# A graph network's lone column group as a 2x2 block product of seven half-width products

## The chip, the cores and the metric

The kernel runs on one core of one Trainium2 chip. The metric is device time of one execution in microseconds (us). The kernel before takes 461.95 us, the median of 3 runs (461.89 to 461.96).

## The reference

2500 nodes with 256 features, 80000 edges sorted by their end node, three layers. Each layer takes, for every node, the mean over its incoming edges of a linear map of (own features, neighbour minus own), and a relu; a last linear map joins the input and the three layers' outputs.

```
h = relu(layernorm(x));  xs = [h]
for W, b in three layers:
    m = concat([h[dst], h[src] - h[dst]]) @ W + b       # 80000 x 512 by 512 x 256
    s = segment_sum(m, dst);  cnt = segment_sum(1, dst)
    h = relu(s / max(cnt, 1));  xs.append(h)
out = x + concat(xs) @ Wf + bf
```

Since m is linear, the kernel never forms it by edge. With A the matrix of counts (how many edges go from node i to node j), s is A-transposed times z, with z = (h W_b) scaled by node, plus h times (W_t - W_b) for nodes that have edges. So a layer is a small product per node (z, and the layer's share of the last map), and a large one with A, 2560 by 2500.

## The kernel before

**Tiles.** Nodes lie in 20 tiles of 128, two of which make one of Q = 10 steps (q). The columns of A (end nodes) are in 5 groups: four of 504 columns, and group 4, `alone`, of 486. Features stand on the partitions in `hT` (256 = 2 x 128 rows, by node). z is held in two parts, `zh` and `zl`, whose sum has the precision of F32; each product with A is done with both, in TensorE's fast F32 form. `sh` and `sl` hold sums of the four 128 x 128 blocks of z, made by `combine` (three DVE operations `tmp<-tmp`) and `Nodes.sums` (ACT's `sh`, DVE's `sl`).

**Layer 0** builds A while it multiplies: the units of group g (`layer`, one per tile of 128, plus four `own` units in between with the product of hT and its own weight) run on TensorE, while group g+1 is compared and counted (`compare`, `counts`, `take_counts`; loop of lines 1120 to 1160). When a group's A is complete, `finish` (lines 903 to 913) adds one row from `cnt` and POOL stores A as bf16 to `a_dram[g]`. `by_count` (915 to 920) scales hT by the counts and, for groups 2 to 4, lets `split_own` (1082 to 1088) split the group's first own factor in three parts: ACT the high one, DVE the low and the cross one. Group 4 builds nothing; in its units `shares` (717 to 737) counts all edges found, by DVE's `fewer` and `found` and one tiny matmul `bank<-ones,found`, and `first_forms` (1094 to 1106) prepares layer 1.

**Layers 1 and 2** (lines 1423 to 1488) have two stages. The *lone stage* goes through the ten q: `Nodes` (1207 to 1239) makes z for two tiles by 12 matmuls of 512 columns from three parts of hT made two steps ahead (`Split`: ACT's `staged<-hT`, then two DVE `staged`); `parts` scales (ACT `tmp` twice), takes the high part (ACT `zh`), the low one (DVE `zl`) and adds the share of the last map to `acc` (DVE, twice). Two steps behind, `Alone.multiply` (1333 to 1371) multiplies z of that step with group 4's columns: 8 matmuls of 486 columns, of a block loaded as bf16 from `a_dram[4]` and cast by ACT (`block<-staged`). Four plain F32 matmuls bring group 4's own part, two of them at the end. The *stream* (`Stream.run`, 1405 to 1413) then multiplies groups 0 to 3, as two pairs (`Pair`, 1246 to 1331). A pair is a 2x2 block product by seven products in place of eight (`SEVEN`): b11, b21, b22 are blocks of A, r1 to r4 sums of blocks that DVE makes (r1 to r2 are cast by ACT after that). Each of 5 chunks gives seven steps of four matmuls of 504 columns, with blocks made LEAD = 5 steps ahead. `take` brings the seven results together.

**What sets the order.** Each engine does its instructions in the order in which the code issues them, and each waits by semaphore for the operands of others, and for those who still read what it overwrites. SP issues the loads, in order too. Nothing is reordered later, so the order of the calls in the loops is the schedule.

## Time and profile before

| | |
|---|---|
| median of 3 runs | 461.95 us (461.89 to 461.96) |
| profiled execution | 461.73 us, of which the span of its instructions is 459.8 |
| group 4 of layer 0, first product | 169.0 us |
| nodes of layer 1, first product | 190.41 us |
| first product of the stream, layer 1 | 238.76 us |
| nodes of layer 2, first product | 315.2 us |
| first product of the stream, layer 2 | 363.57 us |
| last map alone, first product | 439.91 us |
| busy: TensorE / VectorE / ScalarE | 452.0 / 373.7 / 313.0 us |

PE is TensorE's matmul, PEld its weight load, DVE VectorE, ACT ScalarE, POOL GpSimd, SP the engine that issues most transfers. A row of the timeline gives start, duration, engine, line, operation, the names out<-in, the shape and how many, and in brackets how long the engine was idle before it and whom it waited for. The recorded duration of a matmul holds its tail, so the price of one is taken from start to start. A row of stretches gives the busy us of PE, PEld, DVE, ACT and POOL with the number of instructions, then the granted clock of TensorE, the share of the DMA engines and GB/s. Most rows bear line 282, a helper's that records every operation, so places are told by names.

### The profile page before, as it was taken

The numbers are of one execution on the slowest core, as the hardware profiler recorded it, in microseconds if no ns is written. First come the engines' busy times: TensorE is split into PE (matmuls) and PEld (weight loads), VectorE is DVE, ScalarE is ACT, GpSimd is POOL, SyncE is SP. The second block draws the span as 40 slices with busy tenths as digits, with TensorE's granted clock in tenths as the row PEclk, the third lists the DMA queues.
The fourth block names the chain that finished last, engine by engine and source line by source line (L and its number), as shares of the span: only waits on it lengthen the run. The fifth ranks groups of instructions, "written<-read, shape, count | busy, mean of one in ns | idle before, by whom it ended". The sixth has DMA issues, their size and how long they took to land.

```text
span 459.8 us, 7427 instructions
## 1 busy us (share of the span) xinstructions
PE 452.0 (98%) x2729; PEld 356.6 (78%) x2729; DVE 373.7 (81%) x720; ACT 313.0 (68%) x575; POOL 41.6 (9%) x75
## 2 busy tenths in 40 slices
PE   8999999999999999999999999999999999999995
PEld 4888877677778778878878868877788787688685
DVE  7999979899888946199979859886999687569795
ACT  4879878694945434387779839756877897497540
POOL 4770006101001010000000000000000000000000
PEclk9999999999999999999999999999999999999999
DMA  8320088982908249211396522011114855220014
GB/s 273 103 59 13 1 171 133 204 172 42 185 1 168 60 95 189 92 45 45 95 362 235 188 92 91 0 45 46 45 50 138 332 181 180 90 91 0 1 63 165
DMA packets 21784, 52.20 MB, mean 114 GB/s; under 512 B 1915, under 2 KB 12110, under 8 KB 21742
## 3 DMA queue, kind: packets, MB, share of 16 engines
q1 hardware_dynamic: 14110, 33.31, 21.9%
q0 software_dynamic: 5856, 16.48, 18.6%
q10 hardware_dynamic: 1776, 1.89, 1.2%
q8 instruction: 22, 0.36, 0.3%
q14 instruction: 20, 0.16, 0.1%
HBM read 36.21 MB, written 15.62 MB: 113 GB/s over the span
## 4 chain that ended last, share of the span: by engine, by line
PE 96%; DVE 3%; issue 0%; DVEq 0%
PE bank L282 87%; PE pz L282 8%; PE turned L282 1%; DVE one_n L282 1%; DVE one_m L282 1%; DVE own_h L282 0%; DVE hT L282 0%; DVE pick L282 0%; DVE behind L282 0%; DVE deg L282 0%; DVE acc L282 0%; DVE idle L516 0%; DVE acc L431 0%; DVE away L282 0%; DVE deg_b L282 0%
## 5 line engine op out<-in xcount | busy, mean ns | idle before, releaser
L282 ACT CAST block<-staged 128x1008 fp32r<-128x1008 bf16 x120 | 118.0, 1032 | 16.5 <-DVE staged L282 6.5
L282 PE MATMUL bank<-block,zh 128*128 128x504 f32 (+1 forms) x200 | 83.8, 419 | 0.0
L282 PE MATMUL bank<-a,zh 128*128 128x504 f32 (+1 forms) x200 | 82.0, 410 | 0.0
L282 PE MATMUL bank<-a,zl 128*128 128x504 f32 (+1 forms) x200 | 77.8, 389 | 0.0
L282 PE MATMUL bank<-block,zl 128*128 128x504 f32 (+1 forms) x200 | 77.3, 387 | 0.0
L282 ACT CAST a<-bank 128x480 fp32r<-128x480 f32 (+1 forms) x105 | 54.3, 561 | 31.3 <-PE bank L282 31.1
L282 DVE TENSOR_TENSOR one_m<-iota_m,key_m 128x2048 bf16<-128x2048 bf16 (+2 forms) x55 | 64.0, 1164 | 9.4 <-PE bank L282 9.1
L282 PE MATMUL bank<-block,sh 128*128 128x504 f32 x160 | 68.9, 430 | 0.0
L282 PE MATMUL bank<-block,staged 128*128 128x512 f32 (+1 forms) x288 | 62.8, 369 | 0.0
L282 PE MATMUL bank<-block,sl 128*128 128x504 f32 x160 | 62.6, 391 | 0.0
L282 PEld LDWEIGHTS bank<-block,staged 128*128 128x128 f32 x288 | 49.4, 188 | 10.2 <-issue 0.7
L282 DVE TENSOR_TENSOR block<-staged 128x1008 fp32r<-128x1008 bf16 x40 | 46.9, 1204 | 5.2 <-PE bank L282 3.9
L282 PEld LDWEIGHTS bank<-block,zh 128*128 128x128 f32 x200 | 37.6, 188 | 10.9 <-issue 2.5
L282 PEld LDWEIGHTS bank<-block,zl 128*128 128x128 f32 x200 | 37.6, 188 | 10.7 <-issue 3.2
L282 PEld LDWEIGHTS bank<-a,zh 128*128 128x128 f32 x200 | 37.7, 188 | 6.6 <-ACT a L282 0.3
L282 PEld LDWEIGHTS bank<-a,zl 128*128 128x128 f32 x200 | 37.8, 189 | 6.2 <-issue 0.2
L282 DVE TENSOR_TENSOR one_n<-iota_n,key_n 128x640 bf16<-128x640 bf16 (+2 forms) x110 | 42.4, 427 | 0.0
L282 PEld LDWEIGHTS <-one_m 128*128 128x128 bf16 x834 | 30.3, 98 | 13.8 <-issue 7.3
L282 PE MATMUL pz<-wbf,hT 128*128 128x256 f32 x160 | 38.3, 385 | 0.0
L282 PEld LDWEIGHTS bank<-block,sh 128*128 128x128 f32 x160 | 30.1, 188 | 10.3 <-issue 3.5
L282 PEld LDWEIGHTS bank<-block,sl 128*128 128x128 f32 x160 | 30.1, 188 | 9.4 <-issue 3.7
L282 DVE TENSOR_TENSOR staged<-staged 128x1008 bf16<-128x1008 bf16 x40 | 27.1, 678 | 12.0 <-ACT block L282 11.6
(190 smaller groups left out, 633.6 us busy)
## 6 DMA issues: line engine op xcount, KB each, us to landing
staged<-a_dram SPq DMA_DIRECT2D x52, 504.0 KB, 4.4
a_dram<-a POOLq DMA_DIRECT2D x20, 630.0 KB, 9.9
acc<-in_x_dram POOLq DMA_DIRECT2D x3, 640.0 KB, 12.0
out_dram<-acc SPq DMA_DIRECT2D x5, 256.0 KB, 2.2
acc<-in_x_dram SPq DMA_DIRECT2D x2, 512.0 KB
wbf<-in_L_gnn_Wf_dram SPq DMA_DIRECT2D x3, 256.0 KB
acc<-in_x_dram ACTq DMA_DIRECT2D x1, 768.0 KB
wt<-in_L_gnn_W_dram SPq DMA_DIRECT2D x3, 256.0 KB
```

Of the source, the lines that this page charges most:

```text
L282: return self.tc.keep_in_program_order(call(*args, **kwargs))
```

## The change

Group 4's product in layers 1 and 2 becomes a 2x2 block product too, by the same seven products. Its 486 columns are cut into halves of H = 244 (they overlap by two columns), so that a step q has 14 matmuls of 244 columns in place of 8 of 486.

The seven blocks of each q are made once, in layer 0, and kept in DRAM as F32 (`lone_dram`, 976 bytes a row and block): b11, b21, b22 by three transfers that ACT issues in `finish(4)`, the four sums by DVE (`sums_of_alone`), each q's stored by SP. Four of the ten q are done before group 4's products, three of them ahead of `split_own(4, 0)`, the others at odd units of group 4. The sums lie in the buffers of `one_m` and `one_n` in turn, later also in two of their own; each of these must be stored before it is used again. The bf16 copy of group 4, the clearing of its last columns and the ACT casts of its blocks go.

In the lone stage each q's seven blocks (854 KB) are loaded straight to where the matmuls read them. `combine` of the weights and the four sums of hT are made ahead of the stage; the seven own products come at steps 0 and 1. `sums` of a step is issued at the start of the next step, ahead of its `parts`; before, it was behind them. The last of the ten products with group 4 and `end` (the seven `take`) move into the stream, at its step HOLD = 3. `Nodes` uses four banks in turn in place of six. The bodies of `own_sum` and `take` move unchanged from `Pair` to a class `Sevens` that both share.

```diff
-    a_dram = [dram.tile([P, NT, GS], BF16, name=f"a_dram{g}") for g in range(NG)]
+    a_dram = [dram.tile([P, NT, GS], BF16, name=f"a_dram{g}") for g in range(alone)]
+    H = (GWS[alone] * W + 3) // 4 * 2
+    SECOND = slice(GWS[alone] * W - H, GWS[alone] * W)
+    lone_dram = dram.tile([P, Q, 7, H], F32, name="lone_dram")
...
     def finish(g, a):
         c0, n = group_of(g)
-        if n < GS:
-            DVEo.memset(a[:, :, n:].bitcast(F32), 0.0)
         ACTo.copy(a[PAD:PAD + 1, NT - 1, :n], cnt[PAD:PAD + 1, c0:c0 + n])
-        for t in range(0, NT, 5):
-            POOLo.dma_start(a_dram[g][:, t:t + 5, :], a[:, t:t + 5, :].bitcast(F32))
+        if g == alone:
+            halves = a.bitcast(F32).rearrange("p (q h) n -> p q h n", h=2)
+            for h in range(2):
+                ACTo.dma_start(lone_dram[:, :, h, :], halves[:, :, h, :H])
+            ACTo.dma_start(lone_dram[:, :, 2, :], halves[:, :, 1, SECOND])
+        else:
+            for t in range(0, NT, 5):
+                POOLo.dma_start(a_dram[g][:, t:t + 5, :], a[:, t:t + 5, :].bitcast(F32))
...
-        if g > 1:
+        if 1 < g < alone:
...
+    def sums_of_alone(a):
+        def in_two(t, n):
+            return t[:, :2 * n * H].bitcast(F32R).rearrange("p (k n) -> p k n", k=n)
+
+        one_m = hot.tile([P, 2 * BW * CH, P], BF16, name="one_m", bufs=2).rearrange("p k m -> p (k m)")
+        one_n = [hot.tile([P, 2 * BW * (N0 + N1)], BF16, name="one_n", bufs=2) for _ in range(2)]
+        places = [[in_two(one_m, 4)], [in_two(t, 2) for t in one_n]]
+        for q in range(Q):
+            if q == KEPT:
+                places += [[lone_sums.tile([P, 4, H], F32R, name="lone_r")] for _ in range(2)]
+            place = places[q % 2 if q < KEPT else q % 4]
+            r = [t[:, k, :] for t in place for k in range(t.shape[1])]
+            one, two = a[:, 2 * q:2 * q + 2, :H].bitcast(F32), a[:, 2 * q:2 * q + 2, SECOND].bitcast(F32)
+            DVEo.tensor_add(r[0], one[:, 0, :], two[:, 0, :])
+            DVEo.tensor_add(r[1], r[0].bitcast(F32), two[:, 1, :])
+            DVEo.tensor_sub(r[2], one[:, 0, :], r[1].bitcast(F32))
+            DVEo.tensor_add(r[3], r[1].bitcast(F32), one[:, 1, :])
+            k = 3
+            for t in place:
+                SPo.dma_start(lone_dram[:, q, k:k + t.shape[1], :], t.bitcast(F32))
+                k += t.shape[1]
+            yield
+
+    KEPT = 4
...
+            if g == alone and u % 2:
+                next(seven, None)
...
             run(finish(g + 1, a1))
+            if g + 1 == alone:
+                seven = sums_of_alone(a1)
+                for _ in range(KEPT - 1):
+                    next(seven)
+                split_own(alone, 0)
...
+    run(seven)
+    third.close()
...
-    def bank():
-        return next_bank(0, 6)
+    def bank(n=4):
+        return next_bank(0, n)
...
-    tmps = ctx.enter_context(tc.tile_pool(name="tmps", bufs=6))
+    tmps = ctx.enter_context(tc.tile_pool(name="tmps", bufs=3))
...
+    class Sevens:
...
+        def own_factors(self, part, what):
+            one, two = self.one, self.two
+            w = ws[self.l][0][:, part[2], part[1] * P:(part[1] + 1) * P] if part[0] == "x" else wsum[:, part[1], :]
+            m = {"b11": hT[:, 0, one], "b21": hT[:, 1, one], "b22": hT[:, 1, two]}.get(what)
+            return w, self.r[what] if m is None else m
+
...
-    class Alone:
+    class Alone(Sevens):
         def __init__(self, l, order):
             self.l, self.order = l, order
-            self.c0, self.n = group_of(alone)
-            self.to = [ps_left.tile([P, 512], F32, name="bank")[:, :self.n] for _ in range(DC)]
-            self.blocks = {}
-
-        def make(self, p):
-            q = self.order[p]
-            to = self.blocks[p] = block()
-            ACTo.copy(to[:, :, :GS], loaded[p // 2][:, q % 2 * 2:q % 2 * 2 + 2, :])
+            c0, n = group_of(alone)
+            self.one, self.two = slice(c0, c0 + H), slice(c0 + n - H, c0 + n)
+            banks = [ps_left.tile([P, 512], F32, name="bank") for _ in range(4)]
+            self.bank = {what: banks[k // 2][:, k % 2 * 256:k % 2 * 256 + H] for k, (_, what) in enumerate(SEVEN)}
+            self.blocks, self.r, self.free = {}, {}, []
+
+        def temp(self):
+            if not self.free:
+                t = two_tmps()
+                self.free = [t[:, 2 * k:2 * k + 2, :].rearrange("p k n -> p (k n)")[:, :H] for k in range(4)]
+            return self.free.pop(0)
+
+        def load(self, p):
+            st = stage.tile([P, 4 * GS], F32R, name="staged")[:, :7 * H].rearrange("p (k n) -> p k n", k=7)
+            SPo.dma_start(st.bitcast(F32), lone_dram[:, self.order[p], :, :])
+            self.blocks[p] = st
+
+        def own(self, i, j):
+            for k, (part, what) in list(enumerate(SEVEN))[i:j]:
+                PEo.matmul(self.bank[what], *self.own_factors(part, what), start=(k % 2 == 0), stop=False,
+                           skip_group_check=True)
         def multiply(self, p):
-            block = self.blocks.pop(p)
-            for i in range(2):
-                t = 2 * self.order[p] + i
-                for o in range(DC):
-                    for z in (zh, zl):
-                        unit[0] = PEo.matmul(self.to[o], tile_of(z, t)[:, o * P:(o + 1) * P], block[:, i, :self.n],
-                                             start=False, stop=False)
-
-        def own(self, o, c):
-            PEo.matmul(self.to[o], ws[self.l][0][:, c, o * P:(o + 1) * P],
-                       hT[:, c, self.c0:self.c0 + self.n], start=(c == 0), stop=(c == DC - 1))
+            st = self.blocks.pop(p)
+            for k, (part, what) in enumerate(SEVEN):
+                for z in range(2):
+                    unit[0] = PEo.matmul(self.bank[what], part_of(part, z, self.order[p]), st[:, k, :], start=False,
+                                         stop=(p == Q - 1 and z == 1), skip_group_check=True)
         def end(self):
-            for o in range(DC):
-                self.own(o, 1)
-            for o in range(DC):
-                ACTo.activation(hT[:, o, self.c0:self.c0 + self.n], self.to[o], AF.Relu)
-
-    loaded = {}
-
-    def load_alone(k, order):
-        c = order[2 * k] // 2
-        st = stage.tile([P, 8 * GS], BF16, name="staged").rearrange("p (t n) -> p t n", n=GS)[:, :4, :]
-        SPo.dma_start(st, a_dram[alone][:, 4 * c:4 * c + 4, :])
-        loaded[k] = st
+            for _, what in SEVEN:
+                self.take(what)
...
-        def run(self, tick):
+        def run(self, tick, held):
             for n, (m, p, c, part, what, made) in enumerate(self.steps):
+                if n == HOLD:
+                    held()
...
+    HOLD = 3
...
             split(order[2])
         pending = []
         stream = Stream(l)
-        for i in range(Q + LAG):
-            if 0 < i <= Q:
-                lone.make(i - 1)
+        combine(wsum, ws[l][0].rearrange("p c (o n) -> p (c o) n", o=2))
+        for k in range(4):
+            lone.own_sum(k)
+        for i in range(Q + LAG - 1):
+            if pending:
+                pending.pop(0).sums()
             if i < Q:
-                q = order[i]
-                n = Nodes(l, q)
-                n.multiply(splits.pop(q), coming[0])
-                if i + AHEAD_H < Q and i % 2 == 1:
-                    load_alone((i + 1) // 2, order)
+                n = Nodes(l, order[i])
+                n.multiply(splits.pop(order[i]), coming[0])
                 n.parts()
                 n.combine()
-                if i + AHEAD_H < Q and order[i + AHEAD_H] not in splits:
-                    split(order[i + AHEAD_H])
                 pending.append(n)
-            if i and pending:
-                pending.pop(0).sums()
-            if 0 < i <= DC:
-                lone.own(i - 1, 0)
+            if i < 2:
+                lone.own(3 * i, 3 + 4 * i)
             if i >= LAG:
                 lone.multiply(i - LAG)
-            if i == Q - 1:
-                load_alone(Q // 2 - 1, order)
-                stream.load(3)
-        stream.make(2)
-        lone.end()
+            if i < Q:
+                lone.load(i)
+            if i + AHEAD_H < Q and order[i + AHEAD_H] not in splits:
+                split(order[i + AHEAD_H])
+            if i >= Q - AHEAD_H:
+                stream.load(i - Q + AHEAD_H + 1)
+        stream.make(3)
+
+        def held():
+            lone.multiply(Q - 1)
+            stream.load(4)
+            stream.make(5)
+            lone.end()
+
```

DVE at the end of group 3 (`hT<-hT,cnt` is `by_count(4)`; `own_h` the low and cross parts of `split_own(4, 0)`), before:

```order
L282 TENSOR_TENSOR hT<-hT,cnt 128x486 x2
L282 TENSOR_TENSOR own_h_2618<-hT,own_h_2617 128x486
L282 SCALAR_TENSOR_TENSOR own_h_2619<-own_h_2618,own_h_2617 128x486
L282 MEMSET a 128x20x18
L282 TENSOR_SCALAR fewer<-bank 128x20
L282 TENSOR_REDUCE found<-fewer 128x1
```

and after the change, from the third q's sums on (eight more rows of `one_m` and `one_n`, those of the first two, stand between `hT<-hT,cnt` and these):

```order
L282 TENSOR_TENSOR one_m<-a 128x244
L282 TENSOR_TENSOR one_m<-one_m,a 128x244
L282 TENSOR_TENSOR one_m<-a,one_m 128x244
L282 TENSOR_TENSOR one_m<-one_m,a 128x244
L282 TENSOR_TENSOR own_h_2662<-hT,own_h_2661 128x486
L282 SCALAR_TENSOR_TENSOR own_h_2663<-own_h_2662,own_h_2661 128x486
L282 TENSOR_TENSOR one_n<-a 128x244
L282 TENSOR_TENSOR one_n<-one_n,a 128x244
L282 TENSOR_TENSOR one_n<-a,one_n 128x244
L282 TENSOR_TENSOR one_n<-one_n,a 128x244
L282 TENSOR_SCALAR fewer<-bank 128x20
L282 TENSOR_REDUCE found<-fewer 128x1
```

Sixteen additions have come ahead of `found`, and four of them stand behind `own_h`, whose high part ACT makes. On ACT at the same place, after the change (before, `own_h` stood first, ahead of `hT<-bank`, and there were no transfers):

```order
L282 ACTIVATE hT<-bank 128x504 x2
L282 CAST a<-cnt 1x486
L282 DMA lone_dram<-a 1280x1x244 x3
L282 ACTIVATE own_h_2661<-hT 128x486
L282 ACTIVATE own_h_2751<-hT 128x486
```

The high part of `own_h` now stands behind group 3's relu, the row of cnt and the issue of three transfers. At the end of the lone stage of layer 1, ACT before (from the parts of the last but one step on):

```order
L282 ACTIVATE tmp<-bank,share 128x256 x2
L282 CAST zh<-tmp 128x2x256
L282 CAST sh<-tmp 128x512
L282 CAST block<-staged 128x2x504
L282 ACTIVATE tmp<-bank,share 128x256
L282 CAST zh<-tmp 128x2x256
L282 CAST sh<-tmp 128x512
L282 CAST block<-staged 128x2x504
L282 CAST sh<-tmp 128x512
L282 CAST block<-staged 128x2x504 x2
L282 ACTIVATE hT<-bank 128x486 x2
```

and after:

```order
L282 CAST sh<-tmp 128x512
L282 ACTIVATE tmp<-bank,share 128x256 x2
L282 CAST zh<-tmp 128x2x256
L282 CAST sh<-tmp 128x512
L282 ACTIVATE tmp<-bank,share 128x256
L282 CAST zh<-tmp 128x2x256
L282 CAST sh<-tmp 128x512
L282 CAST block<-staged 128x2x504 x6
L282 COPY tmp<-bank 128x244 x2
L282 ACTIVATE hT<-hT 128x2x244 x2
```

The row `sh` that stood behind the next step's `zh` now stands ahead of its `tmp`; it is one step younger than the `sh` before it that shared its place. The casts of lone blocks are gone, and the results of the seven products (`tmp<-bank`, `hT<-hT`) come behind six blocks of the stream.

More of the change, by code (lines that the diff above doesn't have):

```diff
@@ L1136, in by_windows @@
             second.close()
+            third = ctx.enter_context(ExitStack())
+            lone_sums = third.enter_context(tc.tile_pool(name="lone_sums", bufs=2))
             raw_pools.append(ctx.enter_context(tc.tile_pool(name="raw", bufs=1, side="right")))
@@ L1157, in by_windows @@
             run(finish(g + 1, a1))
+            if g + 1 == alone:
[3 more added lines that the diff above has]
+                split_own(alone, 0)
+                next(seven)
             a = a1
         extra = chain(() if g else forms_of_own(), degrees(g + 2) if g + 2 < WG else ())
+    run(seven)
+    third.close()
     first_layer.close()
@@ L1185, in by_windows, with two_tmps @@
     LEAD = 5
+    halves = []
+    def two_tmps():
+        return tmps.tile([P, 8, P], F32, name="tmp")
     def tmp():
-        return tmps.tile([P, 512], F32, name="tmp")
+        if not halves:
+            t = two_tmps().rearrange("p k n -> p (k n)")
+            halves.extend((t[:, :512], t[:, 512:]))
+        return halves.pop(0)[:, :GS]
     def combine(to, x):
@@ L1218, in parts @@
             q = self.q
-            self.zf = tmp()
+            self.both = two_tmps()
+            self.zf, self.raw = (self.both[:, k:k + 4, :].rearrange("p k n -> p (k n)") for k in (0, 4))
             for i, t in enumerate(self.two):
@@ L1233, in combine @@
         def combine(self):
-            self.raw = tmp()
-            combine(self.raw.rearrange("p (s n) -> p s n", s=4), self.zf.rearrange("p (s n) -> p s n", s=4))
+            combine(self.both[:, 4:8, :], self.both[:, 0:4, :])
         def sums(self):
@@ L1250, in __init__ @@
             self.one, self.two = (slice(c0, c0 + n) for c0, n in map(group_of, pairs[i]))
-            self.bank, self.r = {}, {}
+            self.bank, self.r, self.temp = {}, {}, tmp
         def load(self, c):
@@ L1294, in multiply @@
             if c == Q // 2 - 1:
-                if part[0] == "x":
-                    w = ws[self.l][0][:, part[2], part[1] * P:(part[1] + 1) * P]
-                else:
-                    w = wsum[:, part[1], :]
-                m = {"b11": hT[:, 0, self.one], "b21": hT[:, 1, self.one], "b22": hT[:, 1, self.two]}.get(what)
-                PEo.matmul(to, w, self.r[what] if m is None else m, start=False, stop=False)
+                w, m = self.own_factors(part, what)
+                PEo.matmul(to, w, m, start=False, stop=False)
             for k, j in enumerate((2 * c, 2 * c + 1)):
@@ L1397, in make @@
                 m, p, c, part, what, made = self.steps[self.n]
-                if what == "r2":
+                if what == "r2" and m:
                     next(bias, None)
@@ L1427, in by_windows @@
         if l == 1:
-            load_alone(0, order)
             split(order[2])
@@ L1467, in tick @@
                 begun.append(split_in_blocks(6, False))
-            if n == 3:
-                combine(wsum, ws[l][0].rearrange("p c (o n) -> p (c o) n", o=2))
             if n == 40 and l + 1 < L:
@@ L1473, in tick @@
                 split(after[(n - 49) // 7])
-            if n == 63 and l + 1 < L:
-                load_alone(0, after)
             if n in ((65,) if l + 1 < L else (63, 65)):
@@ L1486, in tick @@
                 coming[0].last()
-        stream.run(tick)
+        stream.run(tick, held)
     order = orders[L]
+    turn_of[0] = 0
     for i, q in enumerate(order):
-        po = bank()
-        po = [po[:, :D], bank()[:, :D] if i == Q - 1 else po[:, D:]]
+        po = bank(6)
+        po = [po[:, :D], bank(6)[:, :D] if i == Q - 1 else po[:, D:]]
         for k in range(2):
```

79 lines of the change are left out of this document (39 added, 40 removed).

## The prediction

> **What bounds the kernel now.** I read the page first, then the work of each engine in stretches of 5 us, then the timeline at the three places that the change touches. On the page, these are the busy times and the chain of waits:
>
> ```profile
> PE 452.0 (98%) x2729; PEld 356.6 (78%) x2729; DVE 373.7 (81%) x720; ACT 313.0 (68%) x575; POOL 41.6 (9%) x75
> PE 96%; DVE 3%; issue 0%; DVEq 0%
> ```
>
> TensorE sets the end almost everywhere, so a matmul removed is time removed, as long as TensorE stays fed. How close the others are differs by stage; the stretches are three at the end of layer 0, one of the lone stage of layer 1, and one at its end:
>
> ```profile
> 173.00:178.00 5.00, 5.00 (x24) 4.28 (x23) 3.23 (x5) 2.21 (x4) 0.00 (x0) 1.00 1.05 219
> 178.00:183.00 5.00, 5.00 (x24) 4.26 (x24) 3.62 (x6) 2.88 (x5) 0.00 (x0) 1.00 0.97 198
> 183.00:188.00 5.00, 5.00 (x25) 4.23 (x24) 0.36 (x1) 0.00 (x0) 0.00 (x0) 1.00 0.00 0
> 213.00:218.00 5.00, 5.00 (x23) 4.10 (x23) 4.74 (x11) 3.82 (x7) 0.00 (x0) 1.00 0.00 0
> 233.00:238.00 5.00, 5.00 (x24) 4.09 (x23) 4.20 (x9) 3.93 (x6) 0.00 (x0) 1.00 0.98 358
> ```
>
> PE is at 5.00 of 5.00 in all. But in the lone stage VectorE stands at 4.74 of 5.00: PE leads it by a hair. So this stage can give little, and any new wait of DVE shows.
>
> **What the change saves.** These rows price the products, by their starts:
>
> ```profile
> 229.43 2.95 PE L282 MATMUL bank<-block,staged 128*128 128x512 f32 x12
> 232.22 0.39 PE L282 MATMUL bank<-block,zh 128*128 128x486 f32 x1
> 232.44 0.38 PE L282 MATMUL bank<-block,zl 128*128 128x486 f32 x1
> 237.51 1.79 PE L282 MATMUL bank<-hT,wt 128*128 128x486 f32 x4
> 439.91 5.86 PE L282 MATMUL bank<-block,staged 128*128 128x256 f32 x48
> 445.61 1.89 PE L282 MATMUL bank<-wbf,hT 128*128 128x256 f32 x8
> ```
>
> A 486-wide product takes .22 (232.22 to 232.44), a 256-wide one 5.70/48 = .119 (439.91 to 445.61). A 244-wide one isn't in the trace: between .110 (half of .22) and .122 (no gain over 256 wide, rounded up); I take .115, on the line through both. Per layer 80 x .22 = 17.6 becomes 140 x .115 = 16.1. The own products are plain F32, two records each: 486 wide (1.79 - .57)/3 = .41 a record, .81 a product; 256 wide (1.89 - .38)/7 = .216, .43, so .41 at 244. Four at .81 (3.25) become seven at .41 (2.87). Together -1.9 a layer, **-3.8 us** in all (-1.8 at .122). The casts of blocks that ACT loses (1.03 each) and the stores of A that POOL loses were never waited for, so they give nothing.
>
> **Group 4 of layer 0: a small product behind a long queue.** PE has `bank<-ones,found` after unit 1 of group 4, and everything of PE stands behind it. Before:
>
> ```profile
> 165.45 0.27 ACT L282 CAST a<-bank 128x120 fp32r<-128x120 f32 x1 [0.97 <-PE bank L282]
> 165.60 0.61 ACT L282 ACTIVATE own_h<-hT 128x486 fp32r<-128x486 f32 x1
> 168.74 1.07 ACT L282 ACTIVATE hT<-bank 128x504 f32<-128x504 f32 x2 [2.52 <-PE bank L282]
> 169.84 0.59 ACT L282 CAST a<-cnt 1x486 fp32r<-1x486 bf16 x1
> 170.87 0.17 DVE L282 TENSOR_REDUCE found<-fewer 128x1 f32<-128x20 f32 x1
> 171.63 0.19 PE L282 MATMUL bank<-ones,found 128*1 128x1 f32 x2
> 1.76 0.56 ACTq L282 DMA_DIRECT2D acc<-in_x_dram  x1
> 243.91 0.42 DVE L282 TENSOR_TENSOR wsum<-wt 128x256 f32<-128x256 f32 x1
> staged<-a_dram SPq DMA_DIRECT2D x52, 504.0 KB, 4.4
> out_dram<-acc SPq DMA_DIRECT2D x5, 256.0 KB, 2.2
> ```
>
> `found` is there at 171.04 and PE comes at 171.63. Now it stands behind four sets of sums. A set is four additions of 244 columns, each .42 at most (the 256-wide row), so 1.66. q0 can begin with the last cast of A at 165.7: q0 to 167.4, q1 to 169.0. q2 overwrites what q0's store still reads; 500 KB land in 2.2 (256 KB, queue empty) to 4.4 us (504 KB): q2 at about 171.1, to 172.8. Meanwhile ACT has copied hT (to 169.8) and the row of cnt (170.4), and now issues three transfers of 1280 rows. The one of 768 rows took .56; I estimate .74 each, so 172.6, and own_h's high part only then: 173.2. DVE's low and cross parts, 1.35 (.68 each at 512 columns, the row of `staged` below): 174.6. q3: 176.3. fewer and found, .35: 176.7. PE would be there at 171.6: **+5.1** (3.1 if issues cost nothing and stores land in 2.2, giving 174.8; 7 if a store takes 6).
>
> **The start of layer 1.** Before, DVE is done with layer 0 at 183.4 and idle for 8 us; that slack is now spent. After `found` it has 3.23 + 3.62 + .36 = 7.2 of old work (the windows above) and six more sets, 10.0: 176.7 + 17.2 = 193.9, and about 2 more for waits on stores (3.75 MB of big stores and 5 MB of sums are 24 us at the 358 GB/s of 233 to 238, from about 168 on): 196. The last store lands by the 256 KB row at least 2.2, I take 3, later: 199. Only then does the memory of the sums come free for layer 1's staged parts.
>
> ```profile
> 244.36 0.62 DVE L282 TENSOR_TENSOR wsum<-wsum,wt 128x128 f32<-128x128 f32 x2
> 190.17 1.07 ACT L282 ACTIVATE hT<-bank 128x486 f32<-128x486 f32 x2 [9.14 <-PE bank L282]
> 190.41 2.92 PE L282 MATMUL bank<-block 128*128 128x512 f32 x12
> ```
>
> The split's high part .6 and two DVE steps 1.3 (the rows of `zh` and `staged` below), then wsum 1.05 (.42 + .62): 202. PE starts the nodes at 190.4 + 5.1 = 195.5, has 2.8 for them and .8 for two own products, and at 199.1 wants wsum: **+3.3** (1 with all DMA waits gone; 8 if stores run at the 219 GB/s of 173 to 178).
>
> **The ring in the lone stage.** These are the rows of one step before, and they hold DVE's 4.4 us:
>
> ```profile
> 227.86 0.47 ACT L282 ACTIVATE tmp<-bank,share 128x256 f32<-128x256 f32 x1 [0.93 <-PE bank L282]
> 228.37 0.62 ACT L282 CAST zh<-tmp 128x512 fp32r<-128x512 f32 x1
> 228.90 0.61 ACT L282 CAST sh<-tmp 128x512 fp32r<-128x512 f32 x1
> 226.85 0.68 DVE L282 TENSOR_TENSOR staged<-hT,staged 128x512 fp32r<-128x512 f32 x1
> 228.18 0.68 DVE L282 TENSOR_TENSOR sl<-tmp,sh 128x512 fp32r<-128x512 f32 x1
> 229.03 0.69 DVE L282 TENSOR_TENSOR zl<-tmp,zh 128x512 fp32r<-128x512 f32 x1 [0.17 <-ACT zh L282]
> 229.64 0.87 DVE L282 SCALAR_TENSOR_TENSOR acc<-bank,share,acc 128x256 f32<-128x256 f32 x2
> 230.42 1.07 DVE L282 TENSOR_TENSOR tmp<-tmp 128x256 f32<-128x256 f32 x3
> ```
>
> From `staged` (226.85) to the end of `tmp` x3 (231.49) is 4.64; with the .17 of waiting and the overlaps of starts out, a step is 4.39. Before, `sh` of a step stood behind the next one's `zh` on ACT: nobody waited. Now ACT does `sh` first, and `sh` waits for DVE's `tmp` x3; behind it stand two `tmp` (.47), `zh` (.62), and DVE's `zl` waits for that. From the end of `tmp` x3: .06 + .54 + .49 + .55 + .62 = 2.26, while DVE has staged x2 and `sl`, 2.0. So .23 is lost in each turn, 4.62. PE would need 2.79 + 14 x .115 = 4.40. Over seven steps **+1.6 a layer, 3.2 in all** (0 if PE, at .122 a product, takes 4.50 and DVE's starts overlap more; 4 if each ACT operation is seen .1 later).
>
> **From the lone stage to the stream.** The first block `b11` is cast by ACT behind `sh` of the last step:
>
> ```profile
> 236.14 0.62 ACT L282 CAST sh<-tmp 128x512 fp32r<-128x512 f32 x1 [1.07 <-DVE tmp L282]
> 236.67 1.96 ACT L282 CAST block<-staged 128x1008 fp32r<-128x1008 bf16 x2
> 238.53 0.57 ACT L282 ACTIVATE hT<-bank 128x486 f32<-128x486 f32 x1
> 239.81 5.69 ACT L282 CAST block<-staged 128x1008 fp32r<-128x1008 bf16 x6
> ```
>
> Before, it is done at 237.7, 5.5 after PE's last nodes (229.43 + 12 x .232 = 232.2), and PE has three lone steps (5.3) and the own products (1.6) as cover: no wait. Now the last lone step is in the stream and the own products are at the start, so only two steps of 14 x .115 cover it: 3.2. That alone is a gap of 2.3. With the ring the tail is later: nodes can start when DVE has split their rows; from there DVE has `sl`, the .23, `zl`, acc x2, `tmp` x3 (3.25), then `sh` .6, `sl` .68, the last tile's share .5, `zh` .65, `zl` .68, acc .75, `tmp` x3 1.07, `sh` .65 and the cast 1.03: 9.8. PE has 2.8 + 3.2 = 6.0: a gap of **3.8 a layer, 7.6 in all** (4.6 without the ring's lag).
>
> **The start of the stream.** The last lone step and `end` now come at step 3. There ACT and DVE pass seven results to and fro: two copies .47, eight additions .42, two relu of 488 columns .57 are 5.4 in a chain, with the casts of the next blocks queued behind on ACT. ACT has cast six blocks ahead (.95 each): S + 4.7 for the first product at S; the chain ends at S + 10.2, the next block at S + 11.2. PE needs it after three steps (2.7), the lone step (1.6) and six steps (5.5): S + 9.8. A wait of 1.4, and some .7 for the blocks that DVE adds: **+2.1 a layer, 4.2 in all** (0 if the chain is as short as its ACT part, 1 less ahead; 2.5 a layer if each hand-over costs .1 more).
>
> **Sum**, against the profiled run's 461.73 (span 459.8; the median of the runs is .2 higher): -3.8 + 5.1 + 3.3 + 3.2 + 7.6 + 4.2 = +19.6, **481.3 us**. All low ends together are -3.8 + 3.1 + 1 + 0 + 4.6 + 0 = +4.9 (466.6), all high ends -1.8 + 7 + 8 + 4 + 9 + 5 = +31 (493). They will not all fall one way.
>
> **Rivals.** *The saving shows.* If DVE and ACT run ahead further than the queues say and stores land at once, the gaps close: 461.7 - 3.8 = 457.9. For it: PE waits nowhere today, and DVE has 8 idle us at 183. Against: the gap behind the last nodes needs no DMA, only the order on ACT, and is 2.3 a layer at least, more than the saving. Chance .09.
>
> *The clock falls after the gaps.* PE's first products show a slower rate after idling:
>
> ```profile
> 1.63 4.97 PE L282 MATMUL bank<-idle 128*128 128x512 bf16 x12 [1.63 <-DVE idle L516]
> 6.58 0.81 PE L282 MATMUL turned<-idle 128*128 128x512 bf16 x3
> ```
>
> .41 a product in the first 4.8 us, then (.81 - .38)/2 = .215. If each of the four gaps of 3 to 5 us brought such a stretch, each would cost 2.4. After the gap in group 4 it would only eat the wait at layer 1's start, so three count, and of the two in the stream the waits for blocks swallow about one half: +5, 486. The granted clock in the windows is 1.00 throughout, but PE had no gap there: nothing in the trace speaks against it. Chance .2. The Trainium skill, "TensorE: Matmul & The Clock Gate", section "HAM oscillation", has PE fall to half clock after an idle window of some 3.4 us, and come back after as long a busy one; the two rows above agree with the half rate, and none shows a fall in mid-program. By the page's figure a gap would cost an estimated 1.7 us; it speaks against any change that opens gaps of this length.
>
> *Stores and loads are slower.* The three big stores move pieces of 976 bytes, and no row here shows such. At the 198 to 219 GB/s of the windows from 173 to 183, 8.75 MB take 42 us, not 24: the start of layer 1 waits 8 to 12 rather than 3.3, 488. Chance .08.
>
> *Narrow products run at the plain F32 rate.* If 244 columns fell out of the fast form, .41 each: 280 x .295 = +83, the ring and the gaps behind the nodes covered, 461.7 - 3.8 + 83 + 5 + 3 + 4 = 553. The 256-wide row at .119 speaks against. Chance .04.
>
> **Chances.** Forecast .59, and the rivals .09, .2, .08, .04. The range is 471 to 493: the forecast with half of its bounds, the clock and most of the slow stores, leaving out the two ends. A measurement of this kernel tells .2% (about .9 us) from no change. Faster .1 (the first rival), same .03, slower .87.
>
> **What would show it.** In the profile after: PE idle before `bank<-ones,found`, released by DVE, some 5 us; idle before `bank<-hT,wsum` in layer 1 alone; lone steps of 4.6 from nodes to nodes with short waits for DVE's `staged`; a gap of about 4 before the first `bank<-block,zh` of each stream, released by ACT; 244-wide products .115 apart. I am wrong if the lone stages are shorter than before with no gap behind their last nodes, if 244-wide products take over .15, or if the granted clock falls below 1.00 after a gap.

## The result

The changed kernel takes 485.06 us (median of 4 runs, 484.37 to 486.51) against 461.92 for the kernel before on the same chip: 1.0506 times as long, 95% interval 1.0482 to 1.053. The profiled execution took 485.05 with a span of 483.2; the rest of this text compares that span with the 459.8 of before, 23.4 more.

The page of the changed kernel, its busy times, the granted clock in forty slices, and the chain of waits:

```profile
PE 456.7 (94%) x2861; PEld 363.4 (75%) x2861; DVE 397.5 (82%) x783; ACT 294.1 (61%) x559; POOL 39.8 (8%) x71
PEclk9999999999999977999998999999999899999999
PE 55%; DVE 20%; DMA 12%; ACT 10%; issue 2%; ACTq 0%; DVEq 0%
```

TensorE was 96% of the chain before and is 55% now. Three places in the clock's row lie below full speed, which no slice did before. What PE waited for, as the view of waits has it (us in total, times, longest):

```profile
PE bank L282 <- DVE found L282: 8.7, 1, 8.7
PE bank L282 <- ACT block L282: 8.2, 4, 3.9
PE bank L282 <- issue: 1.2, 1, 1.2
```

The last of these stands before `bank<-hT,wsum`, at the start of layer 1.

Cut at the first product of each stage, the 23.4 lie here (the nodes of layer 2 before start at 315.10, not 315.2):

| stretch | before | after | more |
|---|---|---|---|
| to the nodes of layer 1 | 190.41 | 202.08 | 11.7 |
| lone stage, layer 1 | 48.35 | 51.76 | 3.4 |
| stream, layer 1 | 76.34 | 80.07 | 3.7 |
| lone stage, layer 2 | 48.47 | 49.57 | 1.1 |
| stream, layer 2 | 76.34 | 79.89 | 3.6 |
| last map | 19.89 | 19.83 | -0.1 |

(One lone step, 1.6, has moved from each lone stage to its stream, so the lone stages lose 1.6 more than the rows show, and the streams 1.6 less.) Half of the loss lies ahead of layer 1, in work that only prepares the new product. This is ACT, DVE and PE there, in the timeline of the changed kernel:

```profile
169.81 0.61 ACTq L282 DMA_DIRECT2D lone_dram<-a  x1
171.07 5.86 ACTq L282 DMA_DIRECT2D lone_dram<-a  x2
176.97 0.61 ACT L282 ACTIVATE own_h<-hT 128x486 fp32r<-128x486 f32 x1 [5.93 <-issue]
177.62 0.67 DVE L282 TENSOR_TENSOR own_h<-hT,own_h 128x486 fp32r<-128x486 f32 x1 [5.33 <-ACT own_h L282]
180.65 0.17 DVE L282 TENSOR_REDUCE found<-fewer 128x1 f32<-128x20 f32 x1
180.97 0.19 PE L282 MATMUL bank<-ones,found 128*1 128x1 f32 x2 [8.67 <-DVE found L282]
181.65 0.61 PE L282 MATMUL bank<-a,zl 128*128 128x486 f32 x1
182.06 0.61 PE L282 MATMUL bank<-a,zh 128*128 128x486 f32 x1
```

The order of waits is the one foretold: ACT's `own_h` behind the issue of three stores, DVE behind ACT, `found` behind DVE, PE behind `found`. But the issue is not 3 x .74: the three took .61, .82 and 4.99, so ACT was held until 176.9. And when PE goes on, a 486-wide product takes .41 (181.65 to 182.06), where it took .22 before. The stretches of 5 us show why:

```profile
170.00:175.00 5.00, 2.30 (x27) 1.43 (x26) 1.56 (x4) 1.02 (x2) 0.00 (x0) 1.00 0.97 299
175.00:180.00 5.00, 0.00 (x0) 0.00 (x0) 2.28 (x5) 0.61 (x1) 0.00 (x0) 0.59 1.08 350
180.00:185.00 5.00, 4.03 (x12) 3.37 (x13) 2.98 (x13) 0.22 (x1) 0.00 (x0) 0.50 1.10 320
185.00:190.00 5.00, 5.00 (x22) 4.22 (x21) 3.13 (x7) 1.34 (x2) 0.00 (x0) 0.88 0.87 312
```

The granted clock (the number behind POOL's) falls to .59 while PE idles, is .50 at its return and full again only after 186. DMA moves 299 to 350 GB/s all the while.

The lone stage and its end, in layer 1 (DVE and ACT of one step, then PE at the border to the stream):

```profile
219.90 0.69 DVE L282 TENSOR_TENSOR staged<-hT,staged 128x512 fp32r<-128x512 f32 x1
220.02 0.62 ACT L282 CAST sh<-tmp 128x512 fp32r<-128x512 f32 x1 [2.00 <-DVE tmp L282]
224.44 0.68 DVE L282 TENSOR_TENSOR staged<-hT,staged 128x512 fp32r<-128x512 f32 x1
249.55 0.28 PE L282 MATMUL bank<-staged,zh 128*128 128x244 f32 x1
249.67 0.28 PE L282 MATMUL bank<-staged,zl 128*128 128x244 f32 x1
252.76 3.83 ACT L282 CAST block<-staged 128x1008 fp32r<-128x1008 bf16 x4
253.84 0.50 PE L282 MATMUL bank<-block,zh 128*128 128x504 f32 x1 [3.89 <-ACT block L282]
255.18 0.62 PE L282 MATMUL bank<-block,zh 128*128 128x504 f32 x1
255.60 0.62 PE L282 MATMUL bank<-block,zl 128*128 128x504 f32 x1
```

DVE comes round in 4.54 (219.90 to 224.44), with ACT waiting 2.00 for its `tmp`; before, a step was 4.55, set by PE. So the shorter products buy nothing in the steady step. At its end PE waits 3.9 for the cast of the first block, and then the clock is down again: 504-wide products .42 apart.

### The profile page after: what moved, and what is told of

It is laid out like the page before. It is cut to its first block, busy times and chain, and to the rows that moved or that the text cites. A ratio compares the mean times of both kernels' runs of the same rounds, so it can differ in the third digit from the quotient of the medians.

```text
span 483.2 us, 7823 instructions
## 1 busy us (share of the span) xinstructions
PE 456.7 (94%) x2861; PEld 363.4 (75%) x2861; DVE 397.5 (82%) x783; ACT 294.1 (61%) x559; POOL 39.8 (8%) x71
## 3 DMA queue, kind: packets, MB, share of 16 engines
q0 software_dynamic: 5280, 13.90, 15.0%
q10 hardware_dynamic: 5664, 5.64, 3.7%
## 4 chain that ended last, share of the span: by engine, by line
PE 55%; DVE 20%; DMA 12%; ACT 10%; issue 2%; ACTq 0%; DVEq 0%
PE bank L282 50%; DMA a_dram<-a 9%; DVE tmp L282 5%; PE pz L282 4%; DVE acc L282 3%; DVE zl L282 3%; ACT tmp L282 3%; ACT sh L282 3%; ACT zh L282 2%; DMA acc<-in_x_dram 2%; DVE one_m L282 2%; DVE one_n L282 1%; ACT block L282 1%; DVE hT L282 1%; DVE st L282 1%
## 5 line engine op out<-in xcount | busy, mean ns | idle before, releaser
L282 ACT CAST block<-staged 128x1008 fp32r<-128x1008 bf16 x100 | 96.5, 1030 | 16.9 <-DVE staged L282 10.6
L282 PE MATMUL bank<-block,staged 128*128 128x512 f32 (+1 forms) x288 | 64.5, 373 | 0.0
L282 PE MATMUL bank<-block,zh 128*128 128x504 f32 x120 | 53.5, 446 | 8.2 <-ACT block L282 8.2
L282 PEld LDWEIGHTS bank<-block,staged 128*128 128x128 f32 x288 | 47.4, 188 | 11.2 <-DVE staged L282 3.8
L282 PE MATMUL bank<-block,zl 128*128 128x504 f32 x120 | 48.2, 401 | 0.0
L282 ACT CAST sh<-tmp 128x512 fp32r<-128x512 f32 x20 | 12.4, 621 | 45.4 <-DVE tmp L282 45.4
L282 PE MATMUL bank<-one_n,one_m 128*128 128x60 bf16 x834 | 36.2, 195 | 0.3 <-DVE one_n L282 0.2
```

The source lines that it names most:

```text
L282: return self.tc.keep_in_program_order(call(*args, **kwargs))
```

## The experiments

Times are medians of 4 runs; the kernel before took 461.84 to 462.01 beside them. All are edits of the changed kernel.

**1. POOL issues the large stores (e1_pool).**

```diff
-                ACTo.dma_start(lone_dram[:, :, h, :], halves[:, :, h, :H])
-            ACTo.dma_start(lone_dram[:, :, 2, :], halves[:, :, 1, SECOND])
+                POOLo.dma_start(lone_dram[:, :, h, :], halves[:, :, h, :H])
+            POOLo.dma_start(lone_dram[:, :, 2, :], halves[:, :, 1, SECOND])
```

> The changed kernel, but POOL issues the three large stores of group 4 in place of ACT; nothing else. Theory: the first product after unit 1 of group 4 (bank<-ones,found) was late because ACT sat 5.9 us in the issue of these stores, with the high part of own_h queued behind. Then own_h comes at about 171.0, DVE is through q2 at 172.3, the low and cross parts at 173.7, q3 at 175.3, found at 175.7: the gap of 8.7 falls to about 4, and the whole to 480.5 to 483. Rival: DVE's sums wait for their stores to land (the queue is full of 3.75 MB), whoever issues them; then q3 waits instead, the gap stays over 8 and the time at 484 to 486.

Measured: 482.15. The timeline of this run:

```profile
155.08 0.95 POOL L282 DMA_DIRECT2D lone_dram<-a  x1 [10.72 <-ACT a L282]
170.70 0.61 ACT L282 ACTIVATE own_h<-hT 128x486 fp32r<-128x486 f32 x1
175.01 0.17 DVE L282 TENSOR_REDUCE found<-fewer 128x1 f32<-128x20 f32 x1
175.33 0.19 PE L282 MATMUL bank<-ones,found 128*1 128x1 f32 x2 [3.39 <-DVE found L282]
```

`own_h` and `found` come where the theory had them, within .7, and the gap is 3.4. With the issue off ACT, 5.3 of the 8.7 are gone. The edit moves one thing more: POOL is free early and sends the first of the three stores at 155.08, where ACT sent it at 169.81; it lands 6.4 later, ahead of the sums, so 1.25 of the 3.75 MB no longer stand beside them. The place of `own_h`, right behind the cast of cnt, is due to the issue alone; what the early store adds, this run does not part. Of the 5.3 only 2.9 reached the end: the wait for `wsum` at layer 1's start rose from 1.2 to 2.2 and the clock fell there too. The cure of one wait was half eaten by the next.

**2. `found` early (e2_found_early).** POOL stores as above; the own part is split where it was before the change, and only two sets of sums stand ahead of group 4's units.

```diff
-        if 1 < g < alone:
+        if g > 1:
...
-                for _ in range(KEPT - 1):
-                    next(seven)
-                split_own(alone, 0)
+                next(seven)
                 next(seven)
```

> As the run before, and the own part of group 4 split where it was before the change, with only two of the ten sets of sums ahead of found; the other eight come at odd units of group 4. Theory: found is there before PE, no gap and no fall of the clock there: nodes of layer 1 start at about 191 in place of 202.1. But the stores (8.75 MB from about 168 on) end no earlier than about 195 to 199, and layer 1's parts wait for their memory: the wait before bank<-hT,wsum grows from 1.6 to 5 to 9. The whole 478 to 482. Rival (the sums themselves cost little, only their order did): that wait stays under 3 and the time falls by the full 11, to 474.

Measured: 483.6, above the 478 to 482 of the theory. No wait for `found` is left, the nodes of layer 1 start at 191.44, 10.6 earlier than in the changed kernel. And:

```profile
PE bank L282 <- DVE wsum L282: 8.5, 1, 8.5
PE bank L282 <- ACT block L282: 8.4, 5, 3.8
```

The stream of layer 1 starts at 252.49; in the changed kernel it was 253.84, in run 1 250.70. So wherever PE waits in group 4, layer 1 cannot go on before the sums are made and stored. The order of the queues decides where PE waits, more than how long: the two waits together are 9.9 in the changed kernel, 5.6 in run 1 and 8.5 here. The timeline of this run has both suspects, DVE's additions and a store that a buffer waits for:

```profile
183.84 0.41 DVE L282 TENSOR_TENSOR one_m<-a 128x244 fp32r<-128x244 f32 x1 [5.54 <-DMA lone_dram<-one_m]
201.88 0.63 ACT L282 ACTIVATE staged<-hT 128x512 fp32r<-128x512 f32 x1 [9.03 <-DMA lone_dram<-one_n]
```

DVE idles 5.5 until a buffer's store has landed behind the large ones, and ACT's split for layer 1 waits for the last store.

**3. First blocks of the stream cast early (e3_cast_first).**

```diff
             if i >= Q - AHEAD_H:
                 stream.load(i - Q + AHEAD_H + 1)
-        stream.make(3)
+            if i == Q - 1:
+                stream.make(3)
```

> The changed kernel, but the first three blocks of the stream are cast by ACT at the end of step 9 of the lone stage, ahead of the last sums instead of behind. These blocks need nothing of that step. Theory: the gap before the stream (4.2 and 3.7) is the place of the cast in ACT's queue; it falls to about 1, the granted clock does not fall there, and some 1.9 of it come back a few steps later, where DVE's added blocks are late. Per layer -3 and +1.9 and -1.7 for the clock: 478 to 481. Rival: the gap is a wait for z or for the load of the first chunk; then it stays at about 4 and the time within 1 of 485.

Measured: 481.41, .4 over the range given, with the mechanism as stated. In the timelines of ACT and PE:

```profile
248.58 0.62 ACT L282 CAST zh<-tmp 128x512 fp32r<-128x512 f32 x1 [0.83 <-DVE tmp L282]
249.11 2.90 ACT L282 CAST block<-staged 128x1008 fp32r<-128x1008 bf16 x3
251.91 0.61 ACT L282 CAST sh<-tmp 128x512 fp32r<-128x512 f32 x1
257.53 0.50 PE L282 MATMUL bank<-block,sh 128*128 128x504 f32 x1 [1.39 <-DVE hT L282]
262.75 0.50 PE L282 MATMUL bank<-block,zh 128*128 128x504 f32 x1 [1.00 <-ACT block L282]
```

The gaps before the streams fell from 4.1 and 3.6 to .9 and .4 (the product itself taken off), and no product behind them is slow. 1.4 came back at the fifth step, where DVE's additions for a block are late, and 1.0 at the tenth, where a cast stands behind the seven results on ACT. Cut by stages, the lone stages are 3.3 and 3.2 shorter than in the changed kernel and the streams 1.4 longer each, though their products now go at full rate. Net 3.65.

**4. The gap before the stream filled (e4_fill).**

```diff
...
+            else:
+                for _ in range(18):
+                    PEo.matmul(lone.spare, tile_of(zh, 0)[:, :P], st_last[0], start=False, stop=False,
+                               skip_group_check=True)
```

> The changed kernel with 18 idle products of 244 columns per layer, into an unused half bank, in the gap before the stream (about 2.1 of its 3.7 to 4.2); their results are not read. Theory: the products at .42 in place of .23 at the head of the stream are the clock, that falls after a gap of PE; with the gap filled to about 2 it stays up, and the first eight or nine products of each stream are .23: -1.7 a layer, 481 to 482.5. Rival: they are slow because the loads of the stream take the memory's ports at that time; then they stay at .42 and the time at 485.

Measured: 484.25, over the 481 to 482.5 of the theory. The stretches tell why: layer 1 and layer 2 went differently.

```profile
253.00:258.00 5.00, 4.53 (x14) 3.63 (x15) 3.45 (x5) 5.00 (x6) 0.00 (x0) 0.66 0.12 45
383.00:388.00 5.00, 4.90 (x28) 4.17 (x29) 3.44 (x4) 4.98 (x7) 0.00 (x0) 1.00 0.17 69
```

In layer 2 a gap of 1.6 was left, the clock stayed at 1.00, and the products are .23 apart; in layer 1 a gap of 2.0 was left, and the clock fell as before. The slow products came with the smaller load (45 GB/s) and the fast ones with the larger (69), so the rival of the memory's ports is out: it is the clock. But in layer 2 the wait of PE at the tenth step then grew from .6 to 1.2, so the stream is only .5 shorter. Most of what the clock costs there is hidden by the blocks that would have been late anyway.

**5, 6 and 9. What the wait at layer 1's start is made of (e5_no_sums, e6_no_big_stores, e9_neither).** Run 5 leaves out DVE's additions (SP stores blocks of A in their places), run 6 the three large stores (the loads take sums for the blocks), run 9 both. All are on top of run 2, and the edits are shown against it.

```diff
...
-            DVEo.tensor_add(r[0], one[:, 0, :], two[:, 0, :])
-            DVEo.tensor_add(r[1], r[0].bitcast(F32), two[:, 1, :])
-            DVEo.tensor_sub(r[2], one[:, 0, :], r[1].bitcast(F32))
-            DVEo.tensor_add(r[3], r[1].bitcast(F32), one[:, 1, :])
...
+            SPo.dma_start(lone_dram[:, q, 3:5, :], one)
+            SPo.dma_start(lone_dram[:, q, 5:7, :], two)
```

```diff
-        if g == alone:
-            halves = a.bitcast(F32).rearrange("p (q h) n -> p q h n", h=2)
-            for h in range(2):
-                POOLo.dma_start(lone_dram[:, :, h, :], halves[:, :, h, :H])
-            POOLo.dma_start(lone_dram[:, :, 2, :], halves[:, :, 1, SECOND])
-        else:
+        if g != alone:
...
-            SPo.dma_start(st.bitcast(F32), lone_dram[:, self.order[p], :, :])
+            SPo.dma_start(st[:, 0:3, :].bitcast(F32), lone_dram[:, self.order[p], 3:6, :])
+            SPo.dma_start(st[:, 3:7, :].bitcast(F32), lone_dram[:, self.order[p], 3:7, :])
```

> As e2_found_early, but DVE's forty additions are left out: SP stores blocks of A in the places of the four sums (the same bytes; the products r1 to r4 then have other factors, so the output is another). It tells what the wait of 8.5 at the start of layer 1 is made of. Theory now: it is mainly DVE's 16 us of additions, and its 6 us of waiting for buffers, in front of wsum; without them the wait falls to between 1 and 4 and the whole to 475 to 478. Rival: it is the 8.75 MB of stores; then the wait stays over 6 and the time over 481.

> As e2_found_early, but the three large stores (3.75 MB of the 8.75) are left out, and the loads of layers 1 and 2 take sums in place of the three blocks (two loads a step for one, the same bytes; the output is another). The additions stay. If DVE's additions make the wait at the start of layer 1, it falls by only 1 to 3 (DVE no longer idles 5.5 for a buffer, but has the same work): 480 to 482. If the stores make it, it falls by over 5: under 479.

> As e2_found_early, with both left out: DVE's additions (SP stores blocks of A in their places) and the three large stores (the loads take what is there in place of the three blocks; the output is another). With either left out, the wait at the start of layer 1 fell from 8.5 to 4.2 or 4.4. If the two act in one chain (addition, store, buffer free, next addition), together they account for all of it: the wait falls under 1, the nodes of layer 1 stand as before the change, and the time is 474 to 476.5. If something else of the change holds the start (the order of wsum and the four sums of hT ahead of zl), the wait stays at 3 to 4 and the time at 477 to 478.5.

Measured: 478.56, 478.23 and 472.32. The wait before `wsum` in the views of runs 5 and 6 (in run 9 there is none; the profiled execution of run 6 took 476.74, the shortest of its four):

```profile
PE bank L282 <- DVE wsum L282: 4.2, 1, 4.2
```

```profile
PE bank L282 <- issue: 4.4, 1, 4.4
```

Run 5 came 5.0 under run 2, its wait and its time a little above what the theory gave; run 6 came 5.4 under run 2, where the theory of the additions had 480 to 482. I had expected one of the two to be nearly everything. Together they give 11.3, a little more than the sum and under the range given, and the nodes of layer 1 start at 190.61, where they were before the change (190.41). So it is one chain of both, as the rows of run 2 show it: an addition needs a buffer, the buffer a landed store, the store its turn behind 3.75 MB, and layer 1 the memory behind the last. So half of the loss goes into the making and storing of the blocks. (SP's stores of 5 MB stay in run 9; that they cost nothing there is what its start at 190.61 says.)

**7. Three reorderings together (e7_three).** Runs 1 and 3, and the own products at step 2.

```diff
-            if i < 2:
-                lone.own(3 * i, 3 + 4 * i)
+            if i == 2:
+                lone.own(0, 7)
```

> Three reorderings of the changed kernel together: POOL issues the large stores (as e1_pool), the first blocks of the stream are cast ahead of the last sums (as e3_cast_first), and all seven own products come at step 2 of the lone stage instead of steps 0 and 1, so that wsum is needed 4 us later. If gains add up: 482.15 less 3.65, less up to 1 to 2 at the start of layer 1: 476.5 to 478.5, still well over the 462 of before. If the start of layer 1 only changes what it waits for (the parts for step 2): 478.5.

Measured: 478.91, just over the second figure. The gains of 1 and 3 add up (482.15 - 3.65 = 478.5); bringing `wsum` later gained nothing, since PE waits 1.4 at step 2 instead. It waits not for the split parts, which are done at 202.82, but for a bank: the first `acc<-bank` comes at 205.87, behind `wsum` and the four sums of hT on DVE, PE goes on at 206.45, and `Nodes` now has four banks in turn where it had six.

**8. The sums behind the next parts again (e8_sums_behind).**

```diff
-            if pending:
-                pending.pop(0).sums()
             if i < Q:
...
                 pending.append(n)
+            if i and pending:
+                pending.pop(0).sums()
```

> The changed kernel with the sums of a lone step issued where they were before the change, behind the next step's parts, instead of ahead. It tests the ring. If the ring (DVE's tmp, ACT's sh, tmp, zh, DVE's zl) makes a step 4.54 in place of PE's 4.37, a step is now 4.40 or less, and the gap before the stream shrinks by the ring's lag, to 2.5 to 3: per layer -1.5 and -1.3, the clock falls no more: 478 to 481. Rival: DVE's 4.4 us of work a step, and sl now later, hold PE as much: steps stay at 4.5 to 4.7, the gap is 2 to 2.5 before the last products, and the time 482 to 484.

Measured: 483.91, within the rival's range. The steady steps got longer, 4.68 in place of 4.54, and the timeline of ACT and DVE shows a different ring:

```profile
232.58 0.68 DVE L282 TENSOR_TENSOR sl<-tmp,sh 128x512 fp32r<-128x512 f32 x1
233.35 0.84 ACT L282 ACTIVATE tmp<-bank,share 128x256 f32<-128x256 f32 x2 [2.14 <-DVE sl L282]
234.88 0.69 DVE L282 TENSOR_TENSOR zl<-tmp,zh 128x512 fp32r<-128x512 f32 x1 [0.29 <-ACT zh L282]
```

ACT's `tmp` now waits for DVE's `sl`, which still reads the buffer that `tmp` is to overwrite: the change has three double buffers for `tmp`, one of them held by the sums of hT. So this edit took one ring away and closed another, and the ring of the prediction is not tested by it. What bears on that ring is other. In layer 1 of runs 1, 2, 5 and 6, where PE waits longest at the start and DVE so begins the stage with a lead, all steps from the fourth on take 4.37 to 4.40, PE's own time, though DVE comes round in 4.54 all the same (234.92 to 239.46 in run 1). In run 7 the steps do so too, until they go over to 4.55.

**10. Sums and stores free, and the first blocks early (e10_neither_cast).** Run 9 with the edit of run 3.

> As e9_neither, and the first blocks of the stream cast ahead of the last sums (as e3_cast_first). It tells what the change costs in layers 1 and 2 alone, if the making of the sums were free and the gap before the stream closed. If the rest (ring, blocks of DVE late at the fifth step, the seven results in the stream) is as in e3_cast_first, 470.5 to 473: still over the 462 of before by some 10, so no reordering of the sums alone makes the change pay. If the rest shrinks when the stage starts in step, 465 or less.

Measured: 469.35, somewhat under the first range; its ratio to before is 1.0158 (1.014 to 1.0176). The granted clock is at 90% or more in all forty slices of its page. Even with the additions and the three large stores left out, the kernel is 7.5 us slower than the one before. By stages, against before, the lone stages are .9 and 1.6 shorter and the streams 5.2 and 5.0 longer, of which 1.6 each is the lone step that moved. What PE waits for there:

```profile
PE bank L282 <- ACT block L282: 3.6, 4, 1.0
PE bank L282 <- DVE hT L282: 2.8, 2, 1.4
```

The lone steps stand at DVE's turn, 4.53. No version that beats the kernel before came out of these runs.

## Why the prediction was right

481.3 was forecast, 471 to 493 as the range, and 485.06 measured. The direction and the order of waits came as stated. One of the three signs by which the prediction called itself wrong came too: the granted clock fell below 1.00 after gaps. Term by term:

| step of the prediction | foretold | profile after |
|---|---|---|
| products saved | -3.8 | -4.3 |
| group 4, `found` | +5.1 | +8.7, and 2 to 2.5 of slow products |
| start of layer 1 | +3.3 | +1.2 to 1.6 |
| ring of the lone stage | +3.2 | +1.9 |
| lone stage to stream | +7.6 | +7.7 |
| start of the streams | +4.2 | +4.3: waits 1.2, slow products about 3 |

The right column adds up to 22 of the 23.4. Of the rest, .6 lies ahead of group 4's first product (169.6 against 169.0), and .8 I can't place. That the sum came within 4 us is in part luck: the issue on ACT (3.6 too low) and the slow products in group 4 (2.3, not in the sum) were partly balanced by the start of layer 1, the ring and the products, which came out 1.9, 1.3 and .5 lower.

*The saving* was right: a 244-wide product takes .113 (.115 foretold), so 80 x .22 becomes 140 x .113, -1.8, and the own products 7 x .41 for 4 x .81, -.4; a layer gives -2.2.

*Group 4* was right in its order and mis-sized in one term, the issue of three stores on ACT: 3 x .74 was drawn on from a single issue with nothing before it, while the third took 4.99. Run 1 shows it: with the issue elsewhere `found` came at 175.2, and my sum without the issue's cost would have given about the same.

*The start of layer 1* was too high here, and its sum has a slip: 202 less 199.1 is 2.9, not 3.3. The greater fault is that the two terms are not independent. The later PE comes out of group 4, the less it waits at layer 1: it waits 8.7 and 1.2 in the changed kernel, 3.4 and 2.2 in run 1, 0 and 8.5 in run 2. The prediction added them as if the second would stand at 3.3 for any first; the sum of both was 8.4 foretold and 9.9 measured. Runs 5, 6 and 9 show that what is behind both is one chain of additions and stores, some 11 us with the slow products behind its wait.

*The ring* has the length 4.54, with DVE's wait of .15 and not .23 (ACT's two `tmp` overlap, .83 for both), and PE needed some steps to run into it: summed over the steps above 4.38, 1.1 in layer 1 and .8 in layer 2, and that is at most, since the third step, 4.56, is as long in layer 1 of runs 1, 2, 5 and 6. That this ring and no other holds the step is argued from the rows (DVE's turn of 4.54 in run 1, where PE goes faster, speaks for it) and is not shown by an edit, since run 8 closed another.

*The lone stage to the stream* was right within .3 a layer (3.8 foretold; 4.1 and 3.6), and run 3 shows that it is ACT's order.

*The start of the streams* was right in its sum, 2.15 a layer, and for the wrong reason: only .6 of it is the wait behind the seven results on ACT; the rest is the clock. Run 4 shows the connection: in its layer 2, where the clock did not fall, the wait was 1.2, near the 1.4 foretold. A slow PE gives ACT time.

*The rival of the clock* (chance .2, 486) came true beside the forecast: four stretches were foreseen, three came, after the gaps of 8.8, 4.1 and 3.6 (from start to start, the product taken off). In the streams it took the place of waits that the forecast had counted, so it raised the sum little there. That the one in group 4 would "only eat the wait at layer 1's start" fits the rows (ACT's split there waits for a store to land, and PE then 1.2 for `wsum`), but no run fills that gap alone, and how far it held is not shown. The rival of the slow stores did not come true: DMA moved 299 to 350 GB/s from 170 to 190. The other two did not come at all: no gap closed by itself, and 244-wide products ran in the fast form.

## What to carry to other kernels

A saving on the bound engine is worth what the stage can give back: here VectorE was at 95% of the stretch of the lone stage shown for the kernel before, so 2.2 us a layer less of TensorE had nowhere to go, and each piece of preparation (forty additions, 8.75 MB of stores) lay on engines that had slack only in parts. Add up the preparation where it is done, up to the first reader of the memory that it uses, as one chain; when its order is changed, the waits on such a chain move first of all: runs 1 and 2 took 8.7 out of group 4 in part and in whole, and gained 2.9 and 1.5. And look for a transfer's issue as for an instruction: what stands behind it on its engine can wait until it is through, 5.9 us here.

## What the runs showed of the hardware

**The issue of a large strided store can hold its engine.** ACT's three issues of 1280 pieces of 976 bytes took .61, .82 and 4.99 us, the last while the second was under way (it landed at 183.72); in runs 3, 4 and 8 the third took 4.89 to 4.98. In run 2 POOL's three took .93, .95 and 1.03, but there the first had landed before the others went out. By the packets that the pages count for each queue, the three took 3888 packets on ACT's (5664 less 1776) and 816 on POOL's (6096 less 5280), for the same bytes. Which of the two, the number in flight or the packets, makes the difference, no run here shows. SP's own issues were .32 to 1.0.

**Gaps far under 3.4 us bring the clock down, and not always.** Over the changed kernel and the ten runs, all gaps of PE of 3.4 us and more behind 165 us (21 of them, a product's own time taken off) were followed by products at .41 to .42 in place of .22 to .23 for some 3 to 6 us. Of four between 2.0 and 2.5, three were (2.0 in run 4, 2.4 in run 1, 2.5 in run 8's layer 2), one was not (2.5 in run 8's layer 1). Of those between 1.3 and 1.6, two in run 7 were and the other nine were not; none of .9 to 1.2 standing alone was. Run 8 has the same gap in both layers, at one of the 244-wide products; the next product comes after .22 in layer 1 and after .36 in layer 2, and those behind it .11 and .21 apart:

```profile
251.76 0.38 PE L282 MATMUL bank<-staged,sl 128*128 128x244 f32 x1 [2.20 <-DVE sl L282]
251.98 0.28 PE L282 MATMUL bank<-staged,sh 128*128 128x244 f32 x1
381.09 0.57 PE L282 MATMUL bank<-staged,sl 128*128 128x244 f32 x1 [2.19 <-DVE sl L282]
381.45 0.42 PE L282 MATMUL bank<-staged,sh 128*128 128x244 f32 x1
```

The Trainium skill ("TensorE: Matmul & The Clock Gate", section "HAM oscillation") says that idle gaps over some 3.4 us are to be avoided. The half rate that it gives for the time after such a gap agrees with these runs; as a bound under which a gap is safe, 3.4 does not hold here, where falls were seen from about 1.5 on. The Trainium skill, on the same page in "Part 1: The HAM clock gate", calls the window of 3.4 us free-running. That would fit gaps of one length going both ways, but by itself not a fall after a gap shorter than the window, and no run here shows the window itself.

**What the slow stretch costs depends on who else is late.** It is about 2.3 us of PE's time behind `found`, some of which PE would have waited at layer 1's start. At the head of the stream it took 1.4 to 1.6 by the products and .5 by the stage's length, because blocks were late anyhow (run 4).
